# Attention over edges: three parts of a node's row summed from PSUM by one reduction per group

## The chip, the cores and the metric

The kernel runs on one core of a Trainium2 chip. A core has five engines that run side by side, each with its own queue of instructions: TensorE (PE, matrix products, with weight loads as PEld), VectorE (DVE), ScalarE (ACT), GpSimd (POOL) and SyncE (SP). Matrix products land in PSUM; the other tiles lie in SBUF; tables lie in the chip's main memory (HBM) and are moved by DMA. An engine takes its instructions strictly in order. If one has to wait for another engine, everything behind it on its queue waits too.

The metric is device time in microseconds of one execution. Three timed runs of the kernel before took 15269.26, 15279.0 and 15285.62 us; their median is 15279.0.

## The reference

The input is a graph of 12,500 nodes with 32 features each and 200,000 directed edges, sorted by target node. Four layers follow one another, each with a residual sum and a normalisation over the 32 features. The first is a tensor product over edges. The second has two Chebyshev convolutions and then an attention layer. The third is a gated tensor product over edges, the fourth a plain sum over neighbours. The change is in the attention layer:

```python
def _gatv2(src, dst, h, Ws, bs, Wd, bd, attn, n):
    fs = (h @ Ws + bs).reshape(n, Hh, Dd)      # Hh = 1, Dd = 32
    fd = (h @ Wd + bd).reshape(n, Hh, Dd)
    e = leaky_relu(fs[src] + fd[dst], 0.2)
    logits = einsum('ehd,hd->eh', e, attn)
    m = segment_max(logits, dst, num_segments=n)
    ex = exp(logits - m[dst])
    a = ex / segment_sum(ex, dst, num_segments=n)[dst]
    ft = segment_sum(fs[src] * a[..., None], dst, num_segments=n)
    return leaky_relu(ft, 0.01)
```

For each edge it needs two rows of 32 numbers: `fs` of the source node, which may be anywhere, and `fd` of the edge's own target node. As edges are sorted by target, the second kind ("own rows") comes from few neighbouring nodes at a time.

## The kernel before

Edges are padded to 98 ticks of 2,048. A tick is 16 columns of 128 edges (`C = 16`); each partition holds one edge of a column. Four columns make a group (`U = 4`), so a tick has four groups (`GT = 4`). Nodes lie in blocks of 128, and the targets of a group fall into two neighbouring blocks (`W = 2`), the first of which is `b`. The program has other arms for graphs that are not like this; they are in the code and were not executed.

In the attention stage the source rows are gathered by GpSimd, 16 indirect DMAs per tick (L207), into a tile of which there are four, so that gathers run ahead. Own rows come by matrix products. The table `fd` was split into three bf16 parts whose sum is the fp32 value, and lies in SBUF as `fd3`, with 3 x 32 numbers per node. VectorE makes a one-hot matrix `oht` from the target numbers (L890, two per group), and PE multiplies it with the two blocks of `fd3` (L897, eight matmuls per group). The product for a group is a PSUM tile `pf` of 128 partitions x 4 columns x 3 parts x 32 numbers. There is one such tile, so the matmuls of the next group wait until it has been read.

The tick's work is three functions in `attend`:
- `prep` makes the one-hots and own rows, adds the three parts to `z` (L908, L909), adds the gathered rows (L910), applies the leaky ReLU (L911), multiplies by `attn` (L912), and sums over the 32 features to the logits `lg` (L914). These are split into bf16 parts and transposed to `lt` for `main`. When the one-hots of a tick are complete, SyncE writes all of them (1 MB) to HBM as `kept` for the next layer (L905).
- `main` spreads the logits along rows with PE (`pr`, L930), makes a penalty `pen` from the one-hots on ScalarE (L933), and updates the running maximum of each node on VectorE with eight custom instructions (`junk`, L940), with small copies `mo` and `mx` before and after.
- `post` subtracts the maximum (`m`, `pm` and `lm`, L947 to L959), takes the exponential, multiplies the gathered rows to `ft` (L962), splits them into bf16 parts on ScalarE and VectorE alternately (L486 to L489), transposes the one-hots (`po`, L969, and the copy `oh`, L972), and adds the products `ps` to the nodes' sums `acc` (L980, L985).

`straight_on` calls `post` of one tick, `main` of the next and `prep` of the one after, and then starts the gathers of a later tick. The order of instructions within an engine's queue isn't written out in this stage: a scheduler at build time mixes the three functions. It places the register loads too: before an instruction whose address depends on the block number `b`, the engine's sequencer reads that number from SBUF (L222), on VectorE eight times per tick.

In `prep`, the middle of the path from PSUM to `z` is this: ScalarE copies each group's `pf` from PSUM to an SBUF tile of the same name, for all 16 columns, and after the four copies VectorE makes two sums over the whole tick. The next layer has a step of the same kind that already works on PSUM: `rows` (L1122) sums its tile `pd` with one reduction per group to `xe`.

Of the kernel before, what the change touches and what calls it, by code (L numbers as in the profile page):

```python
# [11 lines left out]
F32 = mybir.dt.float32  # L12
# [6 lines left out]
ALU = mybir.AluOpType  # L19
AX = mybir.AxisListType  # L20
# [5 lines left out]
P = 128  # L26
N, E, D, M = 12500, 200000, 32, 8
# [6 lines left out]
U, GT = 4, 4  # L34
C = U * GT
# [444 lines left out]
def split3(nc, pool, name, y, shape, y3=None):  # L480

    *outer, n = shape
    if y3 is None:
        y3 = pool.tile([P, *outer, 3, n], BF16, name=f"{name}3")
    r = pool.tile([P, *outer, n], F32, name=f"{name}r")
    nc.scalar.copy(y3[:, :, 0, :], y)  # L486
    nc.vector.tensor_tensor(r, y, y3[:, :, 0, :], op=ALU.subtract)  # L487
    nc.scalar.copy(y3[:, :, 1, :], r)
    nc.vector.tensor_tensor(y3[:, :, 2, :], r, y3[:, :, 1, :], op=ALU.subtract)  # L489
    return y3  # L490
# [33 lines left out]
def kernel(ctx: ExitStack, tc: tile.TileContext, a: dict, out: bass.AP):  # L524
    nc = tc.nc
# [25 lines left out]
    with tc.tile_pool(name="l0a", bufs=1) as outer:  # L551
        acc = outer.tile([P, NB, D + 1], F32, name="acc")
        with tc.tile_pool(name="l0", bufs=1) as one, tc.tile_pool(name="l0w", bufs=2) as work:
# [85 lines left out]
            with tc.tile_pool(name="l0ps2", bufs=2, space=PSUM) as psum:  # L639
                per = 14  # L640
                for b in range(0, NB, per):
                    ps = psum.tile([P, per, D + 1], F32, name="pn")
# [111 lines left out]
    with tc.tile_pool(name="l1", bufs=1) as one, ExitStack() as after:  # L754
# [119 lines left out]
        def attend(name, over, deep):  # L874
# [3 lines left out]
            with tc.tile_pool(name=f"{name}w", bufs=2) as work, \  # L878
# [5 lines left out]
                def prep(s, gx, row):  # L884

                    oht = keep.tile([P, GT, W, U * P], BF16, name="oht")
                    pf = work.tile([P, C, 3, D], F32, name="pf", bufs=1)
                    for q in range(GT):
                        for w in range(W):
                            i = nc.vector.tensor_scalar(  # L890
                                oht[:, q, w, :], row[:, q * U * P:(q + 1) * U * P],
                                ncolf[:, ds((s * GT + q) * W + w, 1)], None, op0=ALU.is_equal)
                        b = gr.block(s * GT + q, [i, *last], (PE,))
                        ps = psp.tile([P, U, 3 * D], F32, name="pf")
                        for u in range(U):
                            for w in range(W):
                                i = nc.tensor.matmul(  # L897
                                    ps[:, u, :], oht[:, q, w, u * P:(u + 1) * P],
                                    fd3[:, ds(b + w, 1)].rearrange("p o k d -> p (o k d)"),
                                    start=(w == 0), stop=(w == W - 1))  # L900
                        last[:] = [i] if isinstance(s, int) or q < GT - 1 else []
                        nc.scalar.copy(pf[:, q * U:(q + 1) * U],
                                       ps.rearrange("p u (k d) -> p u k d", k=3))
                    if isinstance(s, int):
                        nc.sync.dma_start(kept[0][s], oht.rearrange("p q w e -> p (q w e)"))  # L905

                    z = work.tile([P, C, D], F32, name="z", bufs=1)
                    nc.vector.tensor_tensor(z, pf[:, :, 0, :], pf[:, :, 1, :], op=ALU.add)  # L908
                    nc.vector.tensor_tensor(z, z, pf[:, :, 2, :], op=ALU.add)  # L909
                    nc.vector.tensor_tensor(z, z, gx, op=ALU.add)  # L910
                    nc.vector.scalar_tensor_tensor(z, z, 0.2, z, op0=ALU.mult, op1=ALU.max)  # L911
                    nc.vector.tensor_tensor(z, z, attn[:, None, :].to_broadcast([P, C, D]), op=ALU.mult)  # L912
                    lg = keep.tile([P, 1, C], F32, name="lg")
                    nc.vector.tensor_reduce(lg[:, 0, :], z, AX.X, ALU.add)  # L914

                    l3 = split3(nc, work, "l", lg, (1, C))
                    pt = psp.tile([3 * C, P], BF16, name="pt")
                    nc.tensor.transpose(pt, l3.rearrange("p o k c -> p (o k c)"), gr.identb)
                    lt = work.tile([3 * C, P], BF16, name="lt")
                    nc.scalar.copy(lt, pt)  # L920
                    return gx, oht, lg, lt
# [24 lines left out]
                def post(s, gx, oht, lg, mo, mw):  # L946
# [18 lines left out]
                    for q in range(GT):  # L965
# [17 lines left out]
                        for w in range(W):  # L983
                            to = acc3[:, ds(b + w, 1), :].rearrange("p o f -> p (o f)")
                            nc.vector.scalar_tensor_tensor(to, to, mo[:, q * W + w, :], ps[:, w, :],  # L985
                                                           op0=ALU.mult, op1=ALU.add)

                over(prep, main, post)

        def rows_of(t):  # L990
# [10 lines left out]
        for k in (1, 2):  # L1001
# [7 lines left out]
                                op=ALU.mult)  # L1009
# [5 lines left out]
    with tc.tile_pool(name="l2a", bufs=1) as outer:  # L1015
        acc3 = outer.tile([P, NBW, 3 * D], F32, name="acc3")
        nc.vector.memset(acc3, 0.0)
        with tc.tile_pool(name="l2", bufs=1) as one:
# [35 lines left out]
            with tc.tile_pool(name="nv", bufs=1) as np_:  # L1054
# [13 lines left out]
                                        op=ALU.mult)  # L1068
# [405 lines left out]
```

## Time and profile before

| | |
|---|---|
| median of three timed runs | 15279.0 us |
| the profiled execution, its own time | 12416.12 us |
| its span, first to last instruction | 12414.3 us |
| mean granted TensorE clock | 0.650 |
| PE busy in the span | 6894.3 us (56%) |
| VectorE busy | 8007.6 us (65%) |
| ScalarE busy | 2265.0 us (18%) |
| GpSimd busy | 8978.3 us (72%) |
| first and last write of `kept` in the attention stage | 6257.2 and 8370.0 us |
| copies of `pf` on ScalarE (L902) | 392, 187.1 us |
| first sum (L908) and second sum (L909) on VectorE | 98 each, 67.4 and 67.0 us |

The profiled execution is 2863 us shorter than the median of the timed runs; the profile shows only its own execution.

Busy times are shares of one span over stages of different kinds, so what an instruction is worth is read from its own stage, here the stretch from about 6250 to 8390 us. In a group's line stand the source line, engine, operation and tile, the count, then busy time in us and mean duration in ns of one, then the idle time of the engine just before and what ended it. A line with "q" after the engine is work of the engine's sequencer, such as a register load or the issue of a DMA.

### The profile page before, as it was taken

The numbers are of one execution on the slowest core, as the hardware profiler recorded it, in microseconds if no ns is written. First come the engines' busy times: TensorE is split into PE (matmuls) and PEld (weight loads), VectorE is DVE, ScalarE is ACT, GpSimd is POOL, SyncE is SP. The second block draws the span as 40 slices with busy tenths as digits, with TensorE's granted clock in tenths as the row PEclk, the third lists the DMA queues.
The fourth block names the chain that finished last, engine by engine and source line by source line (L and its number), as shares of the span: only waits on it lengthen the run. The fifth ranks groups of instructions, "written<-read, shape, count | busy, mean of one in ns | idle before, by whom it ended". The sixth has DMA issues, their size and how long they took to land.

```text
span 12414.3 us, 148816 instructions
## 1 busy us (share of the span) xinstructions
PE 6894.3 (56%) x43970; PEld 4738.4 (38%) x43971; DVE 8007.6 (65%) x16037; ACT 2265.0 (18%) x4775; POOL 8978.3 (72%) x8869
## 2 busy tenths in 40 slices
PE   3444445000000678787855555554777777777767
PEld 2333334000000345454444444442555555555544
DVE  5655555899500221222268888887999999999932
ACT  0000000000000000000045555551222222222200
POOL 6777776688877657575667777764888888888755
PEclk7677777555555899899956555665555555555579
DMA  5511110333100678687744444442222222222267
GB/s 161 186 51 16 17 17 13 87 87 80 34 0 0 185 202 243 189 239 209 210 111 137 135 134 139 134 134 83 73 73 76 76 73 77 76 73 73 68 180 197
DMA packets 870038, 1350.45 MB, mean 109 GB/s; under 512 B 341368, under 2 KB 554232, under 8 KB 822570
## 3 DMA queue, kind: packets, MB, share of 16 engines
q1 hardware_dynamic: 336172, 748.84, 18.0%
q10 hardware_dynamic: 269348, 470.52, 11.6%
q0 software_dynamic: 263680, 120.99, 8.8%
q8 instruction: 395, 6.47, 0.2%
q14 instruction: 443, 3.63, 0.1%
HBM read 1009.91 MB, written 329.73 MB: 108 GB/s over the span
## 4 chain that ended last, share of the span: by engine, by line
DVE 30%; PE 17%; POOL 12%; DMA 12%; issue 8%; ACT 3%; DVEq 2%; SPq 0%; ACTq 0%; POOLq 0%
DMA m<-matrix 9%; DVE r L1210 6%; PE d L691 6%; POOL matrix L415 5%; DVE p L1187 4%; DVE eq L438 3%; DVE n L399 2%; POOL p L1203 2%; POOL g L1357 2%; PE pf L897 2%; DMA g<-table,src 1%; PE pw L1177 1%; PE ps L980 1%; DVEq L222 1%; POOL g L715 1%
## 5 line engine op out<-in xcount | busy, mean ns | idle before, releaser
L715 POOL DMA_INDIRECT g<-table,src x1760 | 1675.9, 952 | 904.2 <-issue 518.8
L691 PE MATMUL d<-m,y 128*96 128x512 fp8e4 x7350 | 1804.9, 385 | 405.1 <-DMA m<-matrix 379.4
L207 POOL DMA_INDIRECT g<-table,src x1568 | 1589.2, 1014 | 593.2 <-issue 450.1
L1357 POOL DMA_INDIRECT g<-table,src x1568 | 1565.7, 999 | 499.2 <-issue 271.8
L207 POOL DMA_INDIRECT g<-in_x_dram,src x1568 | 1578.0, 1006 | 476.4 <-issue 437.1
L621 PE MATMUL psT<-oh,ft 128*113 128x256 f32 x3136 | 910.2, 461 | 1196.0 <-POOL ft L577 1113.1
L415 POOL DMA_INDIRECT matrix<-val,idx x1056 | 1194.9, 1132 | 364.4 <-issue 362.9
L1210 DVE TENSOR_REDUCE r<-p 128x96 f32<-128x1536 f32 x784 | 1364.9, 1741 | 11.5 <-POOL p L1203 11.5
L241 DVE TENSOR_TENSOR acc<-acc,ps 128x192 f32 x440 | 153.5, 349 | 1878.1 <-PE ps L238 1823.4
L1203 POOL TENSOR_TENSOR p<-vs,xk 128x384 f32<-128x384 f32 x1078 | 1082.5, 1005 | 336.7 <-ACT vs L1193 313.8
L691 PEld LDWEIGHTS <-y 128*96 128x96 bf16 x7350 | 896.7, 125 | 1080.0 <-issue 524.0
L1177 PE MATMUL pw<-wz,zT 32*128 32x384 f32 x3136 | 1164.8, 910 | 225.4 <-DVE p L1203 184.3
L621 PEld LDWEIGHTS psT<-oh,ft 128*113 128x113 f32 x3136 | 686.2, 223 | 1419.7 <-POOL ft L577 1151.9
L1187 DVE TENSOR_TENSOR p<-pw,h 128x768 f32<-128x768 f32 x784 | 743.7, 949 | 32.6 <-PE pw L1181 20.9
L624 DVE TENSOR_TENSOR accT<-accT,psT 113x256 f32 x392 | 162.2, 414 | 784.3 <-PE psT L621 781.0
L1181 PEld LDWEIGHTS pw<-wv,hT 32*128 32x128 f32 x3136 | 516.4, 327 | 366.5 <-issue 336.9
L1193 ACT COPY vs<-pw 128x256 f32<-128x256 f32 (+1 forms) x588 | 208.3, 354 | 2407.9 <-DVE p L1187 2148.5
L1105 PE MATMUL pd<-xd,kept 128*128 x3136 | 390.7, 252 | 459.0 <-DVE xe L1122 339.7
L940 DVE CUSTOM_DVE_ANT_0 junk<-pen,pr,mo 128x512 bf16<-128x512 bf16 x784 | 568.7, 744 | 77.9 <-PE pf L897 46.7
L471 PE MATMUL ps<-ident,most 128*1 128x128 f32 x1 | 0.4, 372 | 1088.9 <-DVE most L469 1088.9
L1177 PEld LDWEIGHTS pw<-wz,zT 32*128 32x128 f32 x3136 | 391.7, 303 | 479.8 <-issue 159.2
L897 PE MATMUL pf<-fd,oht 128*128 x3136 | 412.1, 243 | 263.3 <-DVE lr L487 131.0
(318 smaller groups left out, 13622.1 us busy)
## 6 DMA issues: line engine op xcount, KB each, us to landing
m<-matrix SPq DMA_DIRECT2D x735, 320.0 KB
m<-matrix ACTq DMA_DIRECT2D x735, 320.0 KB
kept<-kept SPq DMA_DIRECT2D x196, 1024.0 KB
kept<-oht SPq DMA_DIRECT2D x98, 1024.0 KB
kept<-oh ACTq DMA_DIRECT2D x392, 256.0 KB
matrix<-zero ACTq DMA_DIRECT2D x98, 960.0 KB
g<-table,src POOLq DMA_INDIRECT x4896
row<-keyrow SPq DMA_DIRECT2D x64, 1152.0 KB
```

The costliest lines, as they stand in the source:

```text
L207: nc.gpsimd.indirect_dma_start(out=g[:, c, :], out_offset=None, in_=table[:, :], in_offset=bass.IndirectOffsetOnAxis(ap=src[:, t * C + c:t ...
L415: i = nc.gpsimd.indirect_dma_start(out=to, out_offset=bass.IndirectOffsetOnAxis(ap=idx[:, t:t + 1], axis=0), in_=of[:, t:t + 1], in_offset ...
L621: nc.tensor.matmul(ps, ft[:, q * U + u, :], oh[:, u, :], start=(u == 0), stop=(u == U - 1))
L691: nc.tensor.matmul(banks[k], y3f[:, b, :], m[:, j:j + n], start=(b == 0), stop=(b == NB - 1 and (h, k) != (0, 0)))
L715: nc.gpsimd.indirect_dma_start(out=g[:, c, :], out_offset=None, in_=table[:, :], in_offset=bass.IndirectOffsetOnAxis(ap=src[:, at:at + 1], ...
L897: i = nc.tensor.matmul(ps[:, u, :], oht[:, q, w, u * P:(u + 1) * P], fd3[:, ds(b + w, 1)].rearrange("p o k d -> p (o k d)"), start=(w == 0 ...
L940: nc.vector.tensor_tensor_reduce(junk, pen[:, w, :], pr, 1.0, mo[:, k, :], op0=ALU.add, op1=ALU.max, accum_out=mw[:, k, :])
L1177: nc.tensor.matmul(pw[:, k, 0:384], t.zT[rows, q, :], wzf[rows, :], start=True, stop=True)
L1187: nc.vector.tensor_tensor(t.p[i][:, :, 0:24, :], t.pw[i][:, :, 0:384].rearrange("p k (o c) -> p k o c", c=16), t.h[:, q, v:v + 2, None, 0: ...
L1203: (nc.vector if here else nc.gpsimd).tensor_tensor(t.p[i][:, k, 24:48, :].rearrange("p (k o) i -> p k o i", k=3), of.rearrange("p (o i) -> ...
L1210: nc.vector.tensor_reduce(t.r[:, 2 * i:2 * i + 2, :], t.p[i], AX.X, ALU.add)
L1357: nc.gpsimd.indirect_dma_start(out=g[:, c, :], out_offset=None, in_=tables[1][:, :], in_offset=bass.IndirectOffsetOnAxis(ap=src[:, at:at + ...
```

## The change

The tile `pf` in SBUF and the four copies into it are gone. After the matmuls of a group, one `tensor_reduce` on VectorE reads the PSUM tile with the part as the innermost axis, adds the three parts, and writes the group's four columns of `z`. `z` is made ahead of the loop over groups, and the two sums over the whole tick are gone. The parts are added in the same order, and everything from the sum with the gathered rows on is as it was.

```diff
                     oht = keep.tile([P, GT, W, U * P], BF16, name="oht")
-                    pf = work.tile([P, C, 3, D], F32, name="pf", bufs=1)
+                    z = work.tile([P, C, D], F32, name="z", bufs=1)
                     for q in range(GT):
...
                         last[:] = [i] if isinstance(s, int) or q < GT - 1 else []
-                        nc.scalar.copy(pf[:, q * U:(q + 1) * U],
-                                       ps.rearrange("p u (k d) -> p u k d", k=3))
+                        nc.vector.tensor_reduce(z[:, q * U:(q + 1) * U, :],
+                                                ps.rearrange("p u (k d) -> p u d k", k=3), AX.X, ALU.add)
                     if isinstance(s, int):
                         nc.sync.dma_start(kept[0][s], oht.rearrange("p q w e -> p (q w e)"))
 
-                    z = work.tile([P, C, D], F32, name="z", bufs=1)
-                    nc.vector.tensor_tensor(z, pf[:, :, 0, :], pf[:, :, 1, :], op=ALU.add)
-                    nc.vector.tensor_tensor(z, z, pf[:, :, 2, :], op=ALU.add)
                     nc.vector.tensor_tensor(z, z, gx, op=ALU.add)
```

Lines of the changed file after this place are three lower than before.

## The prediction

> **What bounds the kernel now.** I read the page's slices first, then one window of the attention stage, the groups of its lines, the timelines of VectorE and SyncE, and the single loads of a register. [...]The window is the steady part of the stage (columns: length; busy time and instructions of PE, weight loads, VectorE, ScalarE, GpSimd; PE clock; DMA share; GB/s):
>
> ```profile
> 6453.00:8332.00 1879.00, 1115.35 (x12673) 890.50 (x12672) 1516.57 (x4988) 1051.47 (x1837) 1427.69 (x1410) 0.60 0.49 136
> ```
>
> SyncE issues one write of one-hots per tick, which gives the tick: (6996.43 - 6910.27) / 4 = 21.54 us.
>
> ```profile
> 6910.27 0.33 SPq L905 DMA_DIRECT2D kept<-oht  x1
> ...
> 6953.22 0.33 SPq L905 DMA_DIRECT2D kept<-oht  x1
> ...
> 6996.43 0.33 SPq L905 DMA_DIRECT2D kept<-oht  x1
> ```
>
> VectorE is busy 1516.57 / 1879 = 81%, or 17.4 us of a tick; 4.1 us are short waits. GpSimd looks nearly as full: each gather takes 1.01 us and 0.29 us pass before the next (451.6 / 1410 adds 0.32), so 16 need about 21 us. But it is released late in the stage by `ft` on VectorE, and gathers lie a tick ahead of their reader, so VectorE's chain sets the pace, with GpSimd just below it. The groups of the window that matter:
>
> ```profile
> L207 POOL DMA_INDIRECT g<-table,src x1410 | 1428.9, 1013 | 451.6 <-issue 405.0 <-DVE ft L962 32.6 <-DMA g<-table,src 8.8
> L902 ACT COPY pf<-pf 128x384 f32<-128x384 f32 x349 | 166.6, 477 | 71.0 <-PE pf L897 69.6
> L908 DVE TENSOR_TENSOR z<-pf 128x512 f32<-128x512 f32 x88 | 60.5, 687 | 1.1 <-ACT pf L902 1.0
> L909 DVE TENSOR_TENSOR z<-z,pf 128x512 f32<-128x512 f32 x88 | 60.1, 684 | 0.0
> ```
>
> L902, L908 and L909 go. The instruction that comes is in this trace already, in the next layer, on the same shape and view:
>
> ```profile
> L1122 DVE TENSOR_REDUCE xe<-pd x392: 539/546/559, 8521.1 to 11779.2; 128x128 f32<-128x384 f32 x196
> ```
>
> VectorE's waits in the second half of a tick (start, length, what; idle before it in brackets):
>
> ```profile
> 6953.48 0.17 DVE L936 COPY mo<-mx 128x2 f32 x1
> 6954.58 0.75 DVE L940 CUSTOM_DVE_ANT_0 junk<-pen,pr,mo 128x512 bf16<-128x512 bf16 x1 [0.93 <-PE pf L897]
> ...
> 6955.92 0.69 DVE L908 TENSOR_TENSOR z<-pf 128x512 f32<-128x512 f32 x1
> ...
> 6957.65 0.69 DVE L910 TENSOR_TENSOR z<-z,g 128x512 f32<-128x512 f32 x1
> 6959.10 0.69 DVE L911 SCALAR_TENSOR_TENSOR z<-z 128x512 f32<-128x512 f32 x1 [0.75 <-DVE z L910]
> ```
>
> The 0.75 and most of the 0.93 are loads of a node-block number into a register (L222), which VectorE's sequencer does between two instructions. At 6953.5, 6957.7 and 6959.2 they took:
>
> ```profile
> L222 DVEq TENSOR_LOAD <-bi x1: 573/573/573, 6953.5 to 6953.5; - x1
> L222 DVEq TENSOR_LOAD <-bi x1: 1031/1031/1031, 6957.7 to 6957.7; - x1
> L222 DVEq TENSOR_LOAD <-bi x1: 303/303/303, 6959.2 to 6959.2; - x1
> ```
>
> Some 0.37 us follow a load until the next instruction goes. The slow ones lie within 5 us of the 1 MB write that SyncE issues at 6953.22; those later take 0.30. That the write is the cause is my reading. The other waits of the tick are 0.44 us for `pm` and, in the split of `ft`, 0.71 and 0.86 us for ScalarE's casts.
>
> **What the Trainium skill says.** "VectorE: DVE Perf Modes", section "The perf-mode tier table", has `tensor_reduce` at one element per cycle; its errata section prices a read from PSUM at 120 cycles plus the elements at 0.96 GHz. For 384 elements that estimate is 525 ns; the row shows 546. "Advanced Engine Details and Errata", "Sequencer Loop", says that a control instruction is executed by the sequencer[...]: the trace agrees, a load under a long instruction costs nothing, one behind a 0.07 us copy is bare. "GPSIMD Engine Reference", "Key points", says that GpSimd shares its SBUF interfaces with VectorE when that reads two SBUF inputs: no run here separates this, but gathers vary.
>
> **The change part by part**, per tick.
>
> Removed on ScalarE: 4 copies x 0.477 = 1.91 us. ScalarE is busy 1051 / 1879 = 56%, and these copies delay VectorE only through `pf`, so this is worth nothing by itself: what hides it is VectorE's own queue.
>
> Removed on VectorE: L908 and L909, 0.61 and 0.60 us from start to next start (6955.92 to 6956.53, 6956.67 to 6957.27). Added: 4 reduces of 0.546; instructions back to back start about 0.08 us before the end of the one before, so 4 x 0.47 = 1.88. Work on VectorE: 1.88 - 1.21 = +0.67 us (+0.81 by full durations).
>
> Moved: the order on each engine is written by the scheduler at build, and the changed program has another. In steady ticks all eight one-hots now stand after the `ft` split, among the `junk` steps, where before three stood between `lg` and `ft`. No DMA is added; the 1 MB write follows the last one-hot and now is issued just ahead of the reduce of group 2. I lay the measured durations along the new order from the end of the `ft` split (time 0):
> - `junk`, `acc`, one-hots, reduces 0: 8 x 0.67, 8 x 0.23, 6 x 0.265, six copies of 0.07, one reduce: 9.7 us. A load stands behind a 0.07 us copy: 0.30 + 0.37 bare, 0.6. End 10.4.
> - Reduce 1, then two one-hots and two small ones, to 11.7. `pf` has one PSUM buffer: the 8 matmuls of group 2 (0.76 us, as in the trace) now wait for VectorE's reduce 1 and not for ScalarE. Reduce 2 starts at 12.0: wait 0.3.
> - The same again for group 3, but the split of the maximum (`m`) lies in it, with ScalarE's casts behind a 1.05 us `pen`: `m` at 12.9. Behind it a load 1.2 us after the write: about 1.0 + 0.37, to 14.3. Reduce 3 starts at 14.4, where its matmuls alone would allow 13.5. Queued behind it are the sum with the gathered rows, leaky, `lg`, and so `ft`, for which PE and the next tick wait.
> - `z` + rows, `lm`, leaky, to 16.3. A load behind the small `lm` starts about 15.7, 4 us after the write: taken as slow, it ends at 17.1; bare 0.7.
> - From `lg` at 17.8 to the end of the `ft` split: 4.5 us, with 0.7 and 0.7 waits for casts, as before.
>
> The sum is 22.3 us against 21.54: +0.75; by terms, work +0.67, waits +0.1 to +0.2. I take +0.8, times 98 ticks = +78 us. Bounds: if neither late load is slow, 1.4 us go, to 20.9, where GpSimd's gathers hold: -0.6 us a tick, -59 us. If a slower PE lengthens both waits for `pf`, +1.5, +147 us.
>
> The profiled execution took 12416.1 us (span 12414.3), so 12494. The median of the runs shown is 15279.0, 2863 us more; no view tells why, and I carry the difference over unscaled: 15279 + 78 = 15357. About 0.2% (31 us, 0.31 us a tick) is what a measurement of this kernel can tell from no change.
>
> **Rivals.**
> - Faster: the late loads are covered. The mechanism is the 1 MB write finishing before them, since it starts earlier against the tail. The tick falls to GpSimd's 20.9 to 21.0: 15279 - 55 = 15224. For: ScalarE loses 1.91 us, loads outside the 5 us take 0.30. Against: the order puts one load 1.2 us behind the write. It decides when the two loads together cost under 0.6 us bare.
> - No change: gathers set the pace in the longer timed runs, where something is slower that the profile does not show; a gather of 1.06 us would do. 15279.
> - Slower still: PE is what the longer runs have slower (0.60 clock granted here). Then each serial wait of reduce, 8 matmuls, reduce grows by 0.3 us, twice, and `pm` behind: +1.4 a tick, 15416.
> - That the reduce is far slower than two adds on this view is excluded by the row of L1122.
>
> **How the numbers follow.** Likeliest 0.58 (15357, its own range 15315 to 15400); faster 0.15; no change 0.13; slower still 0.14. The range from 15230 to 15425 leaves out half of the last and half of the faster case. Faster by over 0.2%: 0.15. Within: 0.13 and a small part of the likeliest, 0.16. Slower: 0.69.
>
> **What would show it.** Right: the groups show 392 reduces of 0.55 us at the new line and no copies of `pf`; VectorE's share of the stage stays at 81 to 82% while the tick grows to about 22.3; PE's `pf` waits for `z`, reduce 2 and 3 wait for `pf`; loads within 5 us of the 1 MB write are slow, and one stands bare ahead of reduce 3. Wrong: a tick under 21.5, GpSimd without waits for `ft`, all late loads at 0.30, or a difference outside the attention stage, which the change does not touch.

## The result, and the profile after

The changed kernel took 15380.13 us (median of six runs, 15365.29 to 15402.58) against 15278.92 us for the kernel before (six runs beside it): +101 us, ratio 1.0066 with an interval of 1.0056 to 1.0076. Slower, as forecast, and 23 us above the forecast 15357.

One fact is needed to read what follows. The same kernel before takes about 12,410 us on some chips and about 15,270 us on others. The comparison above and the trace after are from a chip of the second kind; the trace of before that the prediction read was from the first kind. I call them 12.4 ms chips and 15.3 ms chips and compare only within a kind. The experiments met two chips of each kind, each in one group of runs, so that it is the chip, and not its condition at that time, is not shown. Later runs gave the two missing traces: before on a 15.3 ms chip (run e10_before_again) and after on a 12.4 ms chip (run e4_after).

**After, 15.3 ms chip.** A window of the attention stage (columns: length; busy time and instructions of PE, weight loads, VectorE, ScalarE, GpSimd; PE clock; DMA share; GB/s), and SyncE's writes of one-hots, (9131.76 - 8984.66) / 4 = 36.78 us apart:

```profile
7857.00:10900.00 3043.00, 1170.55 (x11996) 947.98 (x11995) 1455.25 (x4877) 879.45 (x1404) 1266.95 (x1324) 0.52 0.26 79
```

```profile
8984.66 0.33 SPq L905 DMA_DIRECT2D kept<-oht  x1
...
9131.76 0.33 SPq L905 DMA_DIRECT2D kept<-oht  x1
```

VectorE is busy 48% of this stretch, not 81%: 17.6 us of a tick of 36.8. The groups of the window show the reduction with the price that was read from the next layer's row (0.553 us; forecast 0.55), no copies of `pf` on ScalarE, and where the rest of the tick goes (last column: idle time before, and what ended it):

```profile
L207 POOL DMA_INDIRECT g<-table,src x1324 | 1267.2, 957 | 1764.0 <-DVE lr L487 1385.5 <-issue 378.2 <-DMA g<-table,src 0.3
L982 DVE SCALAR_TENSOR_TENSOR acc<-acc,mo,ps 128x99 f32 x663 | 207.3, 313 | 1226.4 <-remote 748.0 <-PE pr L927 414.8 <-PE ps L977 44.6
L902 DVE TENSOR_REDUCE z<-pf 128x128 f32<-128x384 f32 x331 | 183.1, 553 | 60.5 <-PE pf L897 49.7 <-remote 10.7
L933 DVE COPY mo<-mx 128x2 f32 x331 | 55.1, 167 | 108.7 <-issue 108.6
```

VectorE waits ahead of `acc` for 1226 us of this window, 14.8 us a tick in one piece, and GpSimd waits some 16.8 us a tick for VectorE. The engines take turns here.

**Before, 15.3 ms chip.** The same window of the kernel before has the same picture, so the turn-taking belongs to this kind of chip and not to the change:

```profile
L207 POOL DMA_INDIRECT g<-table,src x1371 | 1317.0, 961 | 1740.5 <-DVE ft L962 1348.9 <-issue 391.0 <-DMA g<-table,src 0.6
...
L985 DVE SCALAR_TENSOR_TENSOR acc<-acc,mo,ps 128x99 f32 x684 | 214.8, 314 | 1241.4 <-remote 1181.8 <-issue 37.1 <-PE po L969 6.8
```

One tick of each, by the timelines of VectorE and GpSimd (start, length, what; idle before it in brackets). Before, on a 15.3 ms chip:

```profile
8981.56 0.94 POOL L207 DMA_INDIRECT g<-table,src  x1 [0.30 <-issue]
8985.42 0.32 DVE L985 SCALAR_TENSOR_TENSOR acc<-acc,mo,ps 128x99 f32 x1 [4.05 <-remote]
...
8989.43 0.75 DVE L940 CUSTOM_DVE_ANT_0 junk<-pen,pr,mo 128x512 bf16<-128x512 bf16 x1 [1.25 <-PE pf L897]
...
8997.25 0.69 DVE L962 TENSOR_TENSOR ft<-g,ft 128x512 f32<-128x512 f32 x1
8998.20 0.94 POOL L207 DMA_INDIRECT g<-table,src  x1 [15.70 <-DVE ft L962]
...
9017.19 0.94 POOL L207 DMA_INDIRECT g<-table,src  x1 [0.30 <-issue]
9021.02 0.32 DVE L985 SCALAR_TENSOR_TENSOR acc<-acc,mo,ps 128x99 f32 x1 [4.02 <-remote]
```

After, on a 15.3 ms chip:

```profile
8992.25 0.94 POOL L207 DMA_INDIRECT g<-table,src  x1 [16.86 <-DVE lr L487]
...
9011.18 0.94 POOL L207 DMA_INDIRECT g<-table,src  x1 [0.30 <-issue]
9014.90 0.32 DVE L982 SCALAR_TENSOR_TENSOR acc<-acc,mo,ps 128x99 f32 x1 [14.97 <-PE pr L927]
9015.20 0.55 DVE L902 TENSOR_REDUCE z<-pf 128x128 f32<-128x384 f32 x1
...
9022.08 0.56 DVE L902 TENSOR_REDUCE z<-pf 128x128 f32<-128x384 f32 x1 [0.57 <-PE pf L897]
...
9024.44 0.17 DVE L933 COPY mo<-mx 128x2 f32 x1 [1.28 <-issue]
9024.51 0.55 DVE L902 TENSOR_REDUCE z<-pf 128x128 f32<-128x384 f32 x1
...
9027.97 0.68 DVE L959 TENSOR_TENSOR ft<-g,ft 128x512 f32<-128x512 f32 x1
...
9028.92 0.94 POOL L207 DMA_INDIRECT g<-table,src  x1 [16.80 <-DVE lr L487]
```

A tick has three parts. `ft` has read the old rows, and GpSimd issues 16 gathers (8998.20 to 9018.13; 8992.25 to 9012.12). Some 2.8 us after the last of them VectorE's long wait ends. Then VectorE works up to the next `ft`, and the circle closes: 8985.42 to 8998.20 is 12.78 us before, 9014.90 to 9028.92 is 14.02 us after. Means over the 73 ticks of the steady part:

| 15.3 ms chips | tick | burst of 16 gathers | to the end of VectorE's wait | VectorE's stretch to the next burst |
|---|---|---|---|---|
| before | 35.63 | 19.95 | 2.87 | 12.82 |
| after | 36.78 | 19.89 | 2.75 | 14.14 |

That the parts add up is how they were cut. What they tell is that the first two hardly differ (-0.06 and -0.12 us) and the third grew by 1.32, where the tick grew by 1.15. What the third part holds, as means of the same ticks, each instruction counted up to the start of the next: four reductions of 0.49 us in place of two sums of 0.60 (+0.76), four `acc` where before had two (+0.44), six one-hots where before had five (+0.24), waits of 2.29 against 2.12 (+0.17), and all else -0.29. So a little over half of the growth is the reductions themselves; much of the rest is work that the new order of instructions has placed in this part. By this reading, work that stands in the other part of the tick costs nothing, since VectorE waits out the gathers in any case.

From the first to the last `lg` the stage took 3411.2 us before and 3532.6 after, +121. That profile of before (own time 15242.88) was 34 us under its chip's median of 15276.82, so its 121 and the measured 101 agree within what single executions spread (six runs of after: 37 us).

### The profile page after: what moved, and what is told of

The parts are those of the page before. It is cut to its first block, busy times and chain, and to the rows that moved or that the text cites. A ratio compares the mean times of both kernels' runs of the same rounds, so it can differ in the third digit from the quotient of the medians.

```text
span 15378.5 us, 148780 instructions
## 1 busy us (share of the span) xinstructions
PE 7415.4 (48%) x43970; PEld 5036.4 (33%) x43971; DVE 8008.9 (52%) x16233; ACT 2130.9 (14%) x4383; POOL 8867.7 (58%) x8869
## 4 chain that ended last, share of the span: by engine, by line
DVE 28%; another core or an unknown queue 16%; PE 13%; issue 10%; POOL 6%; DMA 6%; ACT 3%; DVEq 2%; SPq 0%; ACTq 0%; POOLq 0%
DVE r L1207 6%; PE d L691 6%; DMA m<-matrix 5%; POOL matrix L415 4%; DVE p L1184 3%; DVE eq L438 2%; DVE n L399 2%; DVEq L222 2%; PE pw L1174 1%; PE ps L238 1%; PE po L966 1%; DVE xe L1119 1%; PE pf L897 1%; PE ps L1246 1%
## 5 line engine op out<-in xcount | busy, mean ns | idle before, releaser
L715 POOL DMA_INDIRECT g<-table,src x1760 | 1673.4, 951 | 2019.7 <-PE ps L238 523.3
L207 POOL DMA_INDIRECT g<-table,src x1568 | 1502.6, 958 | 2187.3 <-DVE lr L487 1470.2
L691 PE MATMUL d<-m,y 128*96 128x512 fp8e4 x7350 | 2008.3, 416 | 943.9 <-DMA m<-matrix 777.0
L1354 POOL DMA_INDIRECT g<-table,src x1568 | 1564.5, 998 | 517.3 <-issue 271.2
L621 PE MATMUL psT<-oh,ft 128*113 128x256 f32 x3136 | 1020.2, 498 | 1359.1 <-DVE oh L228 616.8
L691 PEld LDWEIGHTS <-y 128*96 128x96 bf16 x7350 | 962.2, 134 | 1650.3 <-issue 1154.4
L621 PEld LDWEIGHTS psT<-oh,ft 128*113 128x113 f32 x3136 | 737.1, 241 | 1641.9 <-issue 1018.8
L982 DVE SCALAR_TENSOR_TENSOR acc<-acc,mo,ps 128x99 f32 x784 | 245.2, 313 | 1385.0 <-remote 879.9
L977 PE MATMUL ps<-ft,oh 128*128 128x99 bf16 x3136 | 312.0, 283 | 1204.9 <-ACT oh L969 741.3
L977 PEld LDWEIGHTS <-oh 128*128 128x128 bf16 x3136 | 268.9, 140 | 1244.4 <-ACT oh L969 757.0
L969 ACT COPY oh<-po 128x1024 bf16<-128x1024 bf16 x392 | 396.6, 1012 | 1775.4 <-remote 1280.3
```

Source lines behind the costliest of these rows:

```text
L207: nc.gpsimd.indirect_dma_start(out=g[:, c, :], out_offset=None, in_=table[:, :], in_offset=bass.IndirectOffsetOnAxis(ap=src[:, t * C + c:t ...
L621: nc.tensor.matmul(ps, ft[:, q * U + u, :], oh[:, u, :], start=(u == 0), stop=(u == U - 1))
L691: nc.tensor.matmul(banks[k], y3f[:, b, :], m[:, j:j + n], start=(b == 0), stop=(b == NB - 1 and (h, k) != (0, 0)))
L715: nc.gpsimd.indirect_dma_start(out=g[:, c, :], out_offset=None, in_=table[:, :], in_offset=bass.IndirectOffsetOnAxis(ap=src[:, at:at + 1], ...
L977: nc.tensor.matmul(ps[:, w, :], oh[:, u, w * P:(w + 1) * P], f3[:, q * U + u].rearrange("p k d -> p (k d)"), start=(u == 0), stop=(u == U ...
L1354: nc.gpsimd.indirect_dma_start(out=g[:, c, :], out_offset=None, in_=tables[1][:, :], in_offset=bass.IndirectOffsetOnAxis(ap=src[:, at:at + ...
```

## The experiments

All times are medians; "before" is the kernel before on the same chip, in the same group of runs.

| run | us | before | ratio (interval) | steady tick | VectorE busy in it |
|---|---|---|---|---|---|
| e0_before (12.4 ms chip) | 12413.77 | 12419.82 | | 21.50 | 17.34 |
| e1_two_pf | 12691.34 | 12419.82 | 1.0222 (1.0204 to 1.0241) | 24.46 | 17.86 |
| e2_two_parts | 12393.51 | 12419.82 | 0.9982 (0.9975 to 0.9989) | 21.35 | 17.20 |
| e3_no_write | 12374.24 | 12419.82 | 0.9967 (0.9957 to 0.9976) | 21.17 | 17.77 |
| e4_after | 12428.24 | 12408.10 | 1.0017 (1.0008 to 1.0025) | 21.87 | 17.69 |
| e8_reduce_sbuf | 12471.07 | 12408.10 | 1.0049 (1.0034 to 1.0065) | 22.17 | 17.97 |
| e6_write_moved | 12377.62 | 12408.10 | 0.9973 (0.9962 to 0.9984) | 21.32 | 17.74 |
| e9_before_write_moved | 12493.45 | 12408.10 | 1.0065 (1.0049 to 1.0080) | 22.40 | 17.28 |
| e10_before_again (15.3 ms chips) | 15242.88 | 15276.82 | | 35.63 | 17.18 |
| e5_act_copies | 15491.45 | 15276.82 | 1.0143 (1.0126 to 1.0160) | 38.02 | 17.76 |
| e11_four_oh | 15354.86 | 15256.61 | 1.0058 (1.0041 to 1.0075) | 36.72 | 17.64 |
| e12_moved_four_oh | 15292.36 | 15256.61 | 1.0021 (1.0014 to 1.0028) | 36.08 | 17.68 |

The steady tick is the mean of 75, by the starts of `lg`; busy time counts overlapping instructions once.

**e0_before**, the kernel before unchanged.

> The kernel before once more, unchanged, for a second profile of it, because the one at hand is 2863 us shorter than the timed runs while the changed kernel's profile has a wait of about 15 us in each tick of the attention stage. Theory A (more work and bare waits on VectorE): the same long wait stands here too, at the same length within 0.3 us, and the rest of a tick is 0.8 to 1.1 us shorter than the changed kernel's. Theory B (the long wait itself has grown): the rest of a tick is equal within 0.3 us and the long wait is about 1 us shorter here.

Of the 12.4 ms kind, with the tick of the trace that the prediction read and no long wait. The expectations of this first group were reckoned from 15380 us; what they say in differences can be judged, the totals can't.

**e4_after**, the changed kernel unchanged, beside before.

> The changed kernel itself, on the chip that the experiments use (the kernel before took 12420 us in the first group of runs, 15279 in the recorded comparison). Theory A (VectorE's chain: more work and a slow register load bare ahead of the copy `mo`): from the two recorded traces, without the one long wait per tick, the tick is 21.9 us against 21.50, so +0.42 us x 98 = +41 us: 12461 us, ratio 1.0033, on a chip where that long wait doesn't occur; reduces 392 x 0.55 us, VectorE busy 17.6 us a tick. Theory B (the long wait is what the change lengthens): no such wait here, so no loss: 12420 +- 10. My prediction's own step (+0.8 us a tick): 12498, ratio 1.0063.

The cost here is +20 us, half of theory A's +41. The steady tick grew as A says, 21.50 to 21.87, which is +36 us over the stage; the first and last ticks gave some 16 back (first to last `lg`: 2104.8 and 2124.7 us, +19.9). At the start of the stage the first gathers are late, and VectorE waits for them less in the changed order. Before (run e0_before, timeline of VectorE):

```profile
6290.22 0.75 DVE L910 TENSOR_TENSOR z<-z,g 128x512 f32<-128x512 f32 x1 [13.57 <-DMA g<-table,src]
...
6310.52 0.69 DVE L910 TENSOR_TENSOR z<-z,g 128x512 f32<-128x512 f32 x1 [11.32 <-DMA g<-table,src]
```

After (run e4_after), in the same place. From the first `lg` on these waits come to 24.9 us before (the two shown) and 10.3 after (with 1.95, 1.18 and 0.46 not shown):

```profile
6296.25 0.69 DVE L907 TENSOR_TENSOR z<-z,g 128x512 f32<-128x512 f32 x1 [6.11 <-DMA g<-table,src]
...
6317.73 0.69 DVE L907 TENSOR_TENSOR z<-z,g 128x512 f32<-128x512 f32 x1 [0.60 <-DMA g<-table,src]
```

So the change costs a fifth as much on this kind as in the recorded comparison, with the same instructions. B, that there is no loss without the long wait, falls for this kind: there is no such wait here, and the steady tick is longer all the same.

**e8_reduce_sbuf**, VectorE's work alone: before, with ScalarE's copies kept and one reduction over SBUF for the two sums.

```diff
-                    nc.vector.tensor_tensor(z, pf[:, :, 0, :], pf[:, :, 1, :], op=ALU.add)
-                    nc.vector.tensor_tensor(z, z, pf[:, :, 2, :], op=ALU.add)
+                    nc.vector.tensor_reduce(z, pf.rearrange("p c k d -> p c d k"), AX.X, ALU.add)
```

> The kernel before with its ScalarE copies kept; only its two sums over SBUF become one reduce of 128x1536 to 128x512, so VectorE's work changes but PE's PSUM buffer is still released by ScalarE. Theory A: the reduce costs some 1.66 to 1.75 us against 1.21 for the two sums, VectorE's work +0.45 to +0.55 a tick; if VectorE's chain passes work on to the tick one for one, 12420 + 49 = 12469 (ratio 1.0039). Rival (the gathers or PE hold the tick, and waits swallow the work): within 10 us of 12420. The build may write another order, which would show in the waits of a tick.

```profile
L908 DVE TENSOR_REDUCE z<-pf 128x512 f32<-128x1536 f32 x85 | 162.6, 1913 | 37.8 <-ACT pf L902 22.7 <-ACT m L488 10.2 <-ACT mo L947 3.1
```

It took 1.91 us, not 1.66 to 1.75. VectorE's busy time per tick rose by 0.63, the tick by 0.67, and the time by 63 us (0.67 x 98 = 66). On a 12.4 ms chip, this work on VectorE passed to the tick nearly one for one. The rival, that gathers or PE hold the tick and swallow it, falls for this kind.

**e2_two_parts**, less work in the same place: each reduction leaves out the third part.

```diff
-                                                ps.rearrange("p u (k d) -> p u d k", k=3), AX.X, ALU.add)
+                                                ps.rearrange("p u (k d) -> p u d k", k=3)[:, :, :, 0:2], AX.X, ALU.add)
```

> The changed kernel with the third of the three parts left out of each reduce, so 256 elements in place of 384; the own rows lose their last bits. A reduce should take 0.55 - 128 / 0.96 GHz = 0.41 us, 0.53 us less work a tick on VectorE in nearly the same order. Theory A, VectorE's queue sets the pace: -52 us against the changed kernel, about 15330. Rival, other engines' waits or the long wait set it: within 10 us of 15380.

```profile
L902 DVE TENSOR_REDUCE z<-pf 128x128 f32<-128x256 f32 x352 | 147.9, 420 | 47.6 <-PE pf L897 45.9 <-issue 1.7
```

128 elements less took 0.132 us less (552 to 420 ns), close to the 0.96 elements per ns that the expectation used. In four reductions that is 0.53 a tick; the tick fell by 0.52 against e4_after and the ratio from 1.0017 to 0.9982. The four shorter reductions still take more of VectorE's time than the two sums did (1.43 against 1.21 us a tick, each instruction counted up to the start of the next). The kernel is faster than before all the same, since VectorE's other instructions take 0.37 us a tick less in the new order. With that order given, the length of the reduction decides the sign.

**e3_no_write**: the changed kernel without the 1 MB write of one-hots; the next layer reads the other kept table, so its sums are of other data.

```diff
-                    if isinstance(s, int):
-                        nc.sync.dma_start(kept[0][s], oht.rearrange("p q w e -> p (q w e)"))
-
...
-                                    nc.sync.dma_start(o, kept[k][t])
+                                    nc.sync.dma_start(o, kept[1][t])
```

> The changed kernel without the 1 MB write of one-hots per tick; the next layer reads the other kept table in its place, with as many bytes, so its own rows are wrong and its traffic is the same. If the write makes the register load ahead of reduce 3 slow (1.0 us against 0.30), all loads take 0.30 and about 0.7 us a tick go: -70 us, 15310. If the write only happens to stand there, the load stays at 1.0 us and the time within 20 us of 15380. If the long wait hangs on this write, some 1400 us go.

The wait behind the load ahead of `mo` fell from 106.5 us to 54.1 in windows of 1879 us (1.24 and 0.61 us a tick), and no load of VectorE took more than 332 ns. In e4_after:

```profile
L933 DVE COPY mo<-mx 128x2 f32 x344 | 57.1, 166 | 106.6 <-issue 106.5
...
L222 DVEq TENSOR_LOAD <-bi x687: 297/303/1115, 6455.2 to 8321.5; - x172
```

In e3_no_write:

```profile
L930 DVE COPY mo<-mx 128x2 f32 x354 | 57.5, 162 | 54.1 <-issue 54.1
...
L222 DVEq TENSOR_LOAD <-bi x711: 297/303/332, 6459.6 to 8330.9; - x178
```

So the loads are slow because of the write, as the prediction read it. The tick fell by 0.70 and the ratio by 0.0050, 62 us, against the 70 expected.

**e6_write_moved**: the changed kernel, all its work kept, with the write issued behind the third `pen` of the next step.

```diff
-                    if isinstance(s, int):
-                        nc.sync.dma_start(kept[0][s], oht.rearrange("p q w e -> p (q w e)"))
...
                         nc.scalar.activation(pen, oht[:, q], AF.Copy, scale=-LOW, bias=LOW)
+                        if isinstance(s, int) and q == 2:
+                            nc.scalar.copy(oht[:, q, 0, 0:2], oht[:, q, 0, 0:2])
+                            nc.sync.dma_start(kept[0][s], oht.rearrange("p q w e -> p (q w e)"))
```

> The changed kernel, with the 1 MB write of the one-hots issued about half a tick later: behind the third masked copy `pen` of the next step, so that VectorE's register loads among the reduces and the tail are over 5 us from it. Same bytes, same work, one 2-element ScalarE copy more a tick. Theory A: the slow load ahead of `mo` becomes a fast one: 0.6 to 0.7 us less a tick, as leaving the write out gave: about 60 us below the changed kernel, 12400 (ratio 0.998 to the kernel before). Rival (it is the queue of transfers, the gathers among them, that the write disturbs, wherever it stands): no gain, within 15 us of the changed kernel. A third outcome: the slow load moves to another load of the `junk` phase, where it is bare as well: same time, and the wait ahead of `junk` grows by 0.7 us.

```profile
L933 DVE COPY mo<-mx 128x2 f32 x352 | 59.2, 168 | 54.8 <-issue 54.6
...
L222 DVEq TENSOR_LOAD <-bi x705: 297/303/327, 6453.1 to 8331.2; - x177
```

The gain of leaving the write out, with the write: 51 us under the changed kernel and 30 under the kernel before, the shortest time of a kernel that does all the work. Neither rival showed: no load of VectorE moved into the 5 us behind the write (in this window the nearest is 8.7 us behind it). The order of VectorE's instructions stayed alike: the wait ahead of `mo` fell by 0.62 us a tick, and no other wait or tile's instructions differ from e4_after by more than 0.06.

**e9_before_write_moved**: the same move in the kernel before.

> The kernel before with the same move of the 1 MB write. Its two slow loads stood ahead of `junk` and behind `z` + rows (waits of 0.87 and 0.65 us a tick at those lines). Theory A: both become fast, 0.6 to 0.9 us a tick less until the gathers hold the tick at 20.9: 12420 - 59 = 12361, ratio 0.995, so that it is faster than both kernels. Rival (gathers disturbed by the write wherever it stands, or a slow load in a new place): 12420 +- 15.

A clear miss: 85 us slower than before, where 59 faster were expected. The part that theory A priced did come: the waits ahead of `junk` and behind `z` + rows fell from 0.86 and 0.65 us a tick to 0.21 and 0.03. But more came elsewhere. The move put other things behind the write. PE's load now follows it by 2.2 to 2.5 us and takes 0.92 us (median of 83 ticks; before it took 0.57), VectorE has a load at 6.3 to 6.9 us that takes 0.3 to 0.9, and waits grew ahead of the first sum, which needs the copies of `pf`, and in the split of `ft`:

```profile
L489 DVE TENSOR_TENSOR ft<-ftr,ft 128x528 bf16<-128x528 f32 x84 | 60.0, 714 | 104.3 <-ACT ft L488 104.3
...
L905 DVE TENSOR_TENSOR z<-pf 128x512 f32<-128x512 f32 x84 | 58.2, 693 | 75.5 <-ACT pf L902 75.5
```

Per tick these are 1.24 us (0.92 in e0_before) and 0.90 (0.01); smaller ones grew ahead of the one-hots (0.45), `mo` and `lr`. That PE's slow load is what makes `pf` late fits the order of the lines but was not tried by itself, and the build wrote another order as well. A theory that priced only VectorE's loads was too narrow.

**e1_two_pf**: two PSUM buffers for `pf` in the changed kernel, and, to make room, one for `pt` and `pm` together.

```diff
-                        ps = psp.tile([P, U, 3 * D], F32, name="pf")
+                        ps = psp.tile([P, U, 3 * D], F32, name="pf", bufs=2)
...
-                    pt = psp.tile([3 * C, P], BF16, name="pt")
+                    pt = psp.tile([3 * C, P], BF16, name="pt", tag="pm")
...
-                    pm = psp.tile([P, C, 3], F32, name="pm")
+                    pm = psp.tile([P, C, 3], F32, name="pm", tag="pm")
```

> The changed kernel with two PSUM tiles pf in place of one; pt and pm share one tile to make room. The matmuls of a group no longer wait for VectorE's reduce of the group before. If the serial waits for pf are a part of the loss (Theory A), 0.5 us a tick come back: about 15330. If they are all of the loss: 15280 or less. If VectorE's added work is all of it: 15370 to 15390. The scheduler's order changes with it.

```profile
L902 DVE TENSOR_REDUCE z<-pf 128x128 f32<-128x384 f32 x306 | 169.2, 553 | 53.4 <-PE pf L897 53.0 <-issue 0.2
...
L487 DVE TENSOR_TENSOR ftr<-ft,ft 128x528 f32<-128x528 f32 x77 | 54.6, 709 | 83.4 <-ACT ft L486 62.8 <-issue 20.7
```

Far slower, and the wait for `pf` didn't even shrink (0.69 us a tick, 0.59 in e4_after). The edit changed two things, and the build laid out another order in which `ftr` waits 1.1 us. Nothing follows for the wait for `pf`.

**e10_before_again**, the trace of before that was missing.

> The kernel before once more, unchanged, to have its trace from the chip of this group. If this is a chip of the recorded comparison's kind (15279 us): the long unnamed wait that the changed kernel showed there once a tick (14.85 us of a tick of 36.78) should stand in this trace too. Theory A (the change acts through VectorE's chain, on top of that wait): tick without the long wait 21.50, as elsewhere, and the long wait within 0.2 us of 14.85. Theory B (a good part of the +101 us is the long wait grown by the change): the long wait is shorter here, by some 0.6 us a tick (60 us / 98). If this is a chip of the other kind: 12410 us, tick 21.50, no long wait, and the question stays open.

It came to a 15.3 ms chip. The tick is 35.63 with 11.9 us of waits longer than 5 us and 2.7 of shorter ones ahead of `acc`: 14.6 in all, where after has 14.8. So B falls again: the long waits are nearly equal in sum. But A as put, that the change acts on top of the wait with the same 0.42, falls as well: the tick grew by 1.15. What replaces both is the table of three parts above.

**e5_act_copies**: the changed kernel with copies on ScalarE that nobody reads.

```diff
+                        spare = work.tile([P, 12, D], F32, name="spare", bufs=1)
+                        nc.scalar.copy(spare, gx[:, 0:12, :])
```

> The changed kernel, with ScalarE given one copy of 128x384 a tick more (of gathered rows, to a tile that nobody reads), a quarter in number of the four copies that the change took from it but without any reader. My prediction's step: ScalarE's time is worth nothing by itself, so this lies within 12 us (0.1%) of the changed kernel: 12428 where the kernel before takes 12410, and 1.0017 as ratio. Rival (ScalarE's freed time had already sped up its casts for the splits of `ft`, `l` and `m`, and so hid part of the loss): the copy delays a cast in some ticks, +0.1 to +0.48 us a tick, +10 to +47 us.

The expectation says one copy a tick; the lines stand in the loop over groups, so there are four, as many as the change took away:

```profile
L905 ACT COPY spare<-g 128x384 f32<-128x384 f32 x320 | 162.0, 506 | 5.5 <-DMA g<-table,src 4.2
```

```profile
L902 DVE TENSOR_REDUCE z<-pf 128x128 f32<-128x384 f32 x320 | 177.7, 555 | 148.8 <-PE pf L897 136.4 <-remote 8.4
...
L909 DVE TENSOR_TENSOR z<-z,g 128x512 f32<-128x512 f32 x80 | 55.4, 692 | 68.3 <-issue 56.2 <-DVE mo L935 10.6 <-DVE m L489 1.5
L935 DVE COPY mo<-mx 128x2 f32 x320 | 52.4, 164 | 48.7 <-issue 29.0 <-DVE mr L487 19.7
```

The ratio rose from the changed kernel's 1.0066 to 1.0143, some 118 us, and VectorE's stretch from 14.14 to 15.6. The wait ahead of the reductions rose from 0.73 to 1.86 us a tick, the one ahead of `mo` fell from 1.31 to 0.61, and one of 0.85 ahead of the sum with the gathered rows came. So on a 15.3 ms chip this much work on ScalarE isn't free, in the order that the build gave it. Since the order changed with it, the run doesn't price the four removed copies; whether ScalarE's time is free on a 12.4 ms chip was not run.

**e11_four_oh**: four buffers for `oh`, to try whether the long wait is for a write to land.

```diff
-                        oh = work.tile([P, U, W * P], BF16, name="oh")
+                        oh = work.tile([P, U, W * P], BF16, name="oh", bufs=4)
```

> The changed kernel with four buffers instead of two for `oh`, the transposed one-hots that ScalarE writes and DMA sends to memory, so that a copy into `oh` waits for the landing of a write of a whole tick ago and not of half a tick ago. Theory C (from the traces of both kernels on a chip where the kernel before takes 15277: the first copy of `oh` of a tick starts 18.3 us after the issue of the third write of the tick before, in both kernels, so a tick is that landing plus the stretch of VectorE's work from there to the next third copy, 17.35 us after the change against 16.29 before): on such a chip the long wait goes, the tick falls from 36.8 to about 21.9 us (VectorE's own pace) and the time by up to 14.9 x 98 = 1460 us, to about 13930, ratio 0.91 to the kernel before. Rival D (the writes as a whole are slow there, some 57 GB/s, and landing grows with the load): the wait comes back at the fourth buffer, the time falls by less than 300 us. On a chip where the kernel before takes 12410 the same interval is 4.4 us and lands in time: no gain by the buffers, 12428 +- 30, the rest being the order that the build writes.

```profile
L969 ACT COPY oh<-po 128x1024 bf16<-128x1024 bf16 x332 | 336.0, 1012 | 1660.2 <-remote 1418.6 <-issue 108.6 <-PE po L966 91.3
```

Theory C falls: tick 36.72, the long wait of VectorE 14.7 us as before. The constant 18.3 us between a write and the copy two later was no landing of the write that held the copy's buffer: with four buffers these copies wait no less (1660 us of the window, 1487 in after). In this trace VectorE's wait ends 2.70 us after the last gather of a burst, as in the others (2.75 and 2.87), wherever the copies of `oh` now stand. Rival D, slow writes as a whole, is not excluded by this run alone, but nothing in it ties a wait to a write.

**e12_moved_four_oh**: both edits, of e6 and of e11.

> Four buffers for `oh` and the 1 MB write moved behind the third `pen` of the next step, in the changed kernel: the candidate that should beat both kernels on either kind of chip. Theory C with theory A: about 60 us under the kernel of the same group with four buffers alone where the order stays alike: 13870 on the slower kind of chip, 12370 on the other (ratio 0.997 to the kernel before there). Rival (the write takes its cost along to another place, or the build writes an order in which ScalarE's copies stand worse): within 20 us of four buffers alone, or slower.

62 us under e11_four_oh, as the move of the write gave 51 on the other kind. The tick fell by 0.65, and VectorE's stretch by 0.66 (14.12 to 13.46): the fast load is worth about the same on both kinds, and on this kind it stands in the stretch that makes up the tick. The level of 13870 was C's and fell with it. At 1.0021 it doesn't beat the kernel before on this kind.

## Why the prediction was right or wrong

**Right in direction and close in size, and in part by errors that cancelled.** Forecast +78; measured +101 on a 15.3 ms chip and +20 on the kind of chip whose trace it read. By its own steps:

- *The reduction's price.* Right: 552 ns (e4_after), 553 (after), against 546 from the next layer's row and the estimate of 525.
- *VectorE's chain sets the pace, with gathers a tick ahead.* Right on the 12.4 ms chips (e8, e2: the tick followed VectorE's work, +0.67 for +0.63 and -0.52 for -0.53). Wrong where the comparison ran: gathers and VectorE take turns, a burst of 19.9 us and then a stretch of VectorE's. The direction survives since VectorE's stretch still counts in full.
- *The walk along the new order.* Nearly right. In e4_after the `ft` split shown ends at 6919.96; from there:

```profile
6930.40 0.56 DVE L902 TENSOR_REDUCE z<-pf 128x128 f32<-128x384 f32 x1
...
6932.16 0.56 DVE L902 TENSOR_REDUCE z<-pf 128x128 f32<-128x384 f32 x1 [0.55 <-PE pf L897]
...
6934.44 0.18 DVE L933 COPY mo<-mx 128x2 f32 x1 [1.19 <-issue]
6934.51 0.55 DVE L902 TENSOR_REDUCE z<-pf 128x128 f32<-128x384 f32 x1
...
6937.36 0.69 DVE L911 TENSOR_REDUCE lg<-z 128x16 f32<-128x512 f32 x1
...
6940.96 0.71 DVE L489 TENSOR_TENSOR ft<-ftr,ft 128x528 bf16<-128x528 f32 x1 [0.71 <-ACT ft L488]
```

  Reduction 1 at 10.4 (forecast 10.4), 2 at 12.2 (12.0), 3 at 14.55 (14.4), behind a `mo` that had waited 1.19 us for a load of 0.90 (about 1.0). Its own matmuls had ended at 6933.94, 0.57 us before it started: it stood behind `mo` in VectorE's queue. PE's matmuls wait for the reduction ahead of them and reduction 2 waits for PE, 0.55 us for 0.3 forecast.
- *The second late load, "taken as slow".* This step failed. It started 4.4 us after the write (6931.57) and took 0.30 us, with no wait behind it:

```profile
L222 DVEq TENSOR_LOAD <-bi x2: 301/302/303, 6936.0 to 6936.7; - x2
```

  In the kernel before, loads 4 to 5 us behind the write took 0.93 to 0.96 us (medians in e0_before); why they are fast at that distance in the new order is not shown. `lg` therefore starts at 17.4 and not 17.8, and from there to the end of the split it is 4.3 us, not 4.5. This tick ends at 21.7, the mean is 21.87, and the forecast was 22.3: +0.37 us instead of +0.8.
- *Work +0.67, waits +0.1 to +0.2.* Measured, each instruction counted up to the start of the next: four reductions 1.96 against two sums 1.21, +0.75; all other VectorE instructions -0.41, since they overlap their neighbours more in the new order; waits +0.03; together +0.37. The walk had most of the -0.41, as without the 0.7 us of the second load it would have ended at 21.6; the sum by terms had put it at nothing.
- *The start of the stage.* Not considered; it gave back 16 us.
- *ScalarE's copies worth nothing.* Not confirmed: in e5_act_copies as many copies without a reader cost 118 us on a 15.3 ms chip, in another order.
- *2863 us "carried over unscaled".* This step failed as well. On a 15.3 ms chip the same edit costs 1.15 us a tick. By the three parts above, only what VectorE does between the end of the gathers' hold and the next burst counts there; all four reductions stand in it, and the new order put two more `acc` and one more one-hot there. That a wait in this stretch counts nearly in full is shown by e12 (the wait ahead of `mo` -0.71, the tick -0.65); that work moved into it does was read from the two traces and not tried by itself. The tick forecast too long for the trace read and the regime left out had opposite signs. That the sum came within 23 us is luck in part, and no proof of either step.

**The rivals.** "Faster" rested on fast late loads: one was fast, the other was not, and the floor of 20.9 never showed (lowest tick 21.17). "No change" had seen that gathers might hold the tick in the longer runs. They do, but one after the other with VectorE and not beside it, so the work is not hidden. "Slower still" put the longer runs down to PE; the waits for `pf` that PE ended are the same 0.6 us a tick on both kinds, so it was not that.

**Of what it asked to see:** 392 reductions at 0.55, VectorE at 81% of the stage in the 12.4 ms trace (1520.37 / 1879), and PE waiting for `z` came. The tick of 22.3 did not. Reduction 3 waits for a load and not for `pf`, and in this order no load of VectorE was slow later than 1.7 us behind the write; the next, from 4.3 us on, took 0.30.

**Open:** why the other engines are held while GpSimd gathers, and 2.8 us more, on the 15.3 ms chips. The three-part reading rests on five traces that agree; a run with fewer or slower gathers would test it.

## What to carry to other kernels

Before moving a sum into the engine that sets the pace, price it in that engine's time alone: a reduction over a short axis cost by the elements read (0.55 us for 384, 0.42 for 256), and ScalarE's copies were not what held this kernel. Then look at the new order as well: here the instructions that nobody edited gave back 0.41 us a tick on one kind of chip, and on the other two `acc` and a one-hot moved to a place where they count, +0.68. A register load behind a short instruction was bare, and a large write issued just ahead of it doubled that wait here; moving the write was worth 51 to 62 us, more than the change in question cost on one kind of chip, but the same move went wrong in another order, so look at every engine's loads behind the write. When the trace and the timed runs differ by a fifth, they are two regimes: cost the change in each.

## What the runs showed of the hardware

- One program takes 12.4 ms on some chips and 15.3 ms on others. On the longer kind VectorE's long wait ended 2.70 to 2.87 us (means of 73 ticks, five traces 2.64 to 2.87) after a burst of gathers had ended, with most of these waits ended by what the profile calls "remote", and the others by PE work long done. In one such wait of e11_four_oh, PE's own timeline shows single matmuls at intervals of some 0.7, 1.4 or 2.1 us (weight loads, left out here, stand between them):

```profile
9002.14 0.24 PE L977 MATMUL ps<-ft,oh 128*128 128x99 bf16 x1 [1.19 <-issue]
9002.87 0.24 PE L977 MATMUL ps<-ft,oh 128*128 128x99 bf16 x1 [0.48 <-issue]
9003.61 0.24 PE L977 MATMUL ps<-ft,oh 128*128 128x99 bf16 x1 [0.50 <-issue]
9005.71 0.26 PE L927 MATMUL pr<-lt,sel 48*128 48x128 bf16 x1 [1.86 <-issue]
```

- A register load from SBUF took 0.30 us, and more behind the issue of a 1 MB write. How far behind differed with the order: in e4_after VectorE's took 0.9 us (up to 1.12) at 1.5 to 1.7 us and 0.30 again from 4.3 us on, and PE's 1.2 at 2.5 us; in e0_before VectorE's took 0.93 to 0.96 at 4 to 5 us (up to 1.15) and 0.30 again from 5.4 us on. Without the write none of VectorE's took more than 0.332 in the window, and none more than 0.327 with the write moved (e6).
- The reduction over SBUF of 128x1536 to 128x512 took 1.91 us, four over PSUM of 128x384 together 2.21 by their durations: 0.3 us more in four pieces from PSUM than in one pass over SBUF.
